# An attention-and-clustering kernel: the last MLP block of the third image computed in pieces during the fourth image's clustering

## The chip, the cores and the metric

The kernel runs on one core of a Trainium2 chip. The metric is the device time of one execution in microseconds (us). Before the change it is 3501.63 us, the median of three runs (3501.41 to 3505.16).

Engines are named as in the profile: PE multiplies matrices (PEld is its weight load), DVE is the vector engine, ACT the scalar engine, POOL the general-purpose engine, SP the engine whose queue issues most transfers. Each works through its own queue in order. Matmul results go to PSUM, everything else lives in SBUF.

## The reference

The input `x` is four images (B = 4) of 256 channels and 64 x 64 pixels, all float32. Two layers follow each other:

```python
# layer 0: attention over N = 4096 pixels
q = wq x + bq ; k = wk x + bk ; v = wv x + bv        # q, k: 32 channels; v: 256
attn = softmax(q k)
x = gamma * (v attn) + x

# layer 1
feat, val = conv1x1(group_norm(x), f_w), conv1x1(group_norm(x), v_w)     # 96 channels each
sim = sigmoid(beta + alpha * cosine(centres(feat), feat))                # per head and quarter image
sim = sim * one_hot(argmax(sim))
agg = (sim val + centres(val)) / (sum(one_hot) + 1)
y = x + ls1 * conv1x1(sim agg, proj_w)
y = y + ls2 * conv1x1(gelu(conv1x1(group_norm(y), mlp_w1)), mlp_w2)      # 256 -> 1024 -> 256
z = relu(batch_norm(y * dw_w))
z = relu(batch_norm(conv1x1(z, pw_w)))                                   # the output
```

Gelu is the tanh approximation, and each group norm runs over a whole image.

## The kernel before

The images go through three stages, one image after another. The order of every engine's instructions is the order of the program text (`manual_schedule`).

**Weighting** (`attention(b).weighting`) is the softmax and its product with `v`: 8 blocks of 512 output pixels by 8 groups of 512 input pixels, 64 units in all. A unit's scores (`score`) are computed 9 units ahead into a buffer of the ring `spool`, tag "s"; `exps` takes the row maximum off, exponentiates, and adds up the denominator on POOL; `weigh` is the product, line 406. Row maxima come from DVE maxima on the scores, `fold`, and `across`, which turns them on PE (`tt`) and builds a diagonal tile `dg` in the pool `work`; `spread` sends it to all partitions (`mb`). In its last units (`ahead`) it loads the next image into four tiles of the ring.

**Clustering** (`cluster`) has many short steps that follow each other: group norm statistics, centres, the products `fv` with the features, similarity (`similar`: a square root on ACT, a Tanh, and then the square root's table again through `table`), the choice of the best centre (`largest`, `weights`), counts (`cnt`), sums (`agg`), transposes (`tp`), projection (`gp`, `op`), and statistics (`seen`, `bn_stats`) for the second group norm. In between, `fill(n)` issues the next `n` pieces of the next image's projections: 32 pieces `v_half` (`vp`), two `k_half` (`kp`), one `q_four` (`qp`). There are 35 pieces; `weighting` takes 8 of them after its last unit, `group_norm` some, `cluster` the rest, and the start of `mlp` (`fill(N)`) whatever remains. The last image has no next one, so its list is empty.

**MLP** (`mlp`) takes the image in 8 blocks of 512 pixels. In a block, `first(nb, j)` computes the hidden groups j and j + 4 (128 channels each) with seven products of 128x256 in place of eight (`hp`, `hu`, `hq`, weights combined beforehand: `w1_s` holds C + D and −D in place of C and D, and `w_abcd`, `w_bac`, `w_bcd` are built on POOL). `second` adds their part of the second layer (`mo`), one group behind. `finish` adds the residue and makes the Relu, `last` does the output layer (`pw`), both one block behind. Evictions of ACT are put off through the list `hooks`, which the next `first` empties. `norm(nb + 1)` prepares the next block at the end of step (nb, 1), with two DVE instructions (line 971) and four subtracts on POOL, into a pair of rows in a ring buffer (`pairs`), which is also the staging buffer of the output transfer.

At the end of step (nb, 2) each block also computes one unit of the next image's scores (`nxt.score(nb, hooks, maxima)`), so that the next weighting finds its first eight units ready. A unit's four DVE maxima are put into `maxima`, and `rest(n)` issues them, two in each call of `first`. After the last block come `fold`, `maximum` (which calls `across`), and the first `exps`.

The ring `spool` has `N // XT + SLOTS` = 14 buffers of 8 KB a partition. It holds the x tiles (two blocks each, 4 an image; an image's tile becomes free when its second block is through `finish` and the Relu), scores, pairs, and the clustering's `vf` and `sim`. The pool `work` has a tag "w" of three rotating buffers (`dg`, `sg`, `cl`, the three combined weights). PSUM is in pools `ps_m` (two buffers), `ps_s` (two buffers of two banks: scores, `hq`, `pw`), and `ps_a` (accumulators).

Of the kernel before, what the change touches and what calls it, by code (L numbers as in the profile page):

```python
# [13 lines left out]
P = 128  # L14
# [3 lines left out]
NB = 512  # L18
# [27 lines left out]
def attention_then_cluster_block(  # L46
# [123 lines left out]
    def derived():  # L170
# [27 lines left out]
        nc.vector.tensor_copy(wf_t, tps[:ED, :C])  # L198
        nc.vector.tensor_copy(fvb[:, :ED], tps[:, C : C + ED])

    probe = const.tile([P, 1], F32, name="probe")
    nc.gpsimd.memset(probe, 1.0)

# [40 lines left out]
    def attention(b, xs):  # L244
# [115 lines left out]
            top = tops[nb]  # L360
            nc.vector.tensor_tensor(top[:, 0], top[:, 0], top[:, 1], ALU.max)

        def across(nb, tag="w", bufs=3):
            top = tops.pop(nb)
            tp = ps_m.tile([P, 4, P], F32, tag="m", name=f"tt_{b}_{nb}")
            for j in range(4):
                nc.tensor.transpose(tp[:, j, :], top[:, 0, j * P : (j + 1) * P], ident)  # L367
            mx = small.tile([P, 4], F32, tag="mx", name=f"mx_{b}_{nb}")
            nc.vector.tensor_reduce(mx, tp, AX.X, ALU.max)
            dg = work.tile([P, 4, P], F32, tag=tag, bufs=bufs, name=f"dg_{b}_{nb}")  # L370
            nc.vector.tensor_tensor(
                dg,
                ident.unsqueeze(1).to_broadcast([P, 4, P]),
                mx.unsqueeze(2).to_broadcast([P, 4, P]),
                ALU.mult,
            )
            return dg
# [108 lines left out]
            score(GRP)  # L486

        def maximum():
            half["dg"] = across(0, "rden", 1)

        def first():
            spread(0, half["dg"])
# [124 lines left out]

    h64_q = h64[:ED].rearrange("p (q h m) -> p q h m", q=4, h=HEADS)

    def cluster(b, ys, stats, cells, rest, fill):  # L620

        pool = small.tile([P, KC, 4, 4], F32, tag="pool", bufs=1, name=f"pool_{b}")

# [90 lines left out]
        ]  # L714
        prns = [small.tile([P, 64], F32, tag="prn", name=f"prn_{b}_{f}") for f in range(2)]

        sgs = [work.tile([P, NB // 2], F32, tag="w", bufs=3, name=f"sg_{b}_{f}") for f in range(2)]
# [14 lines left out]
        def similar(f, meanwhile=lambda: None):  # L732

            sg = sgs[f]
            rsqrt(prns[f], prns[f], L2_EPS, meanwhile)
            nc.vector.tensor_tensor(quad(sg), quad(sg), over_m(prns[f]), ALU.mult)
            nc.scalar.activation(sg, sg, AF.Tanh, scale=ab[:, 0:1], bias=ab[:, 1:2])
            if f == 0:
                table(AF.Sqrt)

        def largest(f):
# [81 lines left out]
        summed(lambda j, q: pool_w[:, j], True)  # L823
        heads(NBLK - 1)
        similar(1, lambda: fill(2))
        fill(3)
        table(AF.Sqrt)
        largest(1)
# [61 lines left out]
        def products(hb, c, qs):  # L890
            if c == 0:
                two = [
                    ps_s.tile([P, 2, NB], F32, tag="s", name=f"op_{b}_{hb}_{c}_{f}")
                    for f in range(2)
                ]
                ops = {q: two[q // 2][:, q % 2, :] for q in qs}
            else:
                ops = {
                    q: ps_a.tile([P, NB], F32, tag=f"a{q % 2}", name=f"op_{b}_{hb}_{c}_{q}")
                    for q in qs  # L900
                }
            for q in qs:
                rows = slice(q * 32, (q + 1) * 32)
                nc.tensor.matmul(  # L904
                    ops[q],
                    g_s[rows, c * P : (c + 1) * P],
                    sim_t[rows, hb, :],
                    start=True,
                    stop=True,
                )  # L910
            for q in qs:
                y = pieces[hb, c, q] = ys[2 * (q // 2) + hb][:, c, :].rearrange(
                    "p (h f w) -> p f h w", h=16, f=2
                )[:, q % 2]
                if c == 0:
                    nc.vector.scalar_tensor_tensor(
                        y,
                        ops[q].rearrange("p (h w) -> p h w", h=16),
                        par("ls1", c),
                        y,  # L920
                        ALU.mult,
                        ALU.add,
                    )
                else:
                    add = work.tile([P, NB], F32, tag="w", bufs=3, name=f"cl_{b}_{hb}_{q}")
# [19 lines left out]
        return stats2  # L945


    def mlp(b, ys, stats2, fill, nxt):


        w_bcd, w_bac, w_abcd = (
            work.tile([P, HID // 2], F32, tag="w", bufs=3, name=f"{n}_{b}")
            for n in ("w_bcd", "w_bac", "w_abcd")
        )
        nc.gpsimd.tensor_tensor(w_abcd, W_CD, W_A, ALU.subtract)
        nc.gpsimd.tensor_tensor(w_bac, w_abcd, W_D, ALU.add)
# [80 lines left out]
        def first(nb, j, todo):  # L1037


            e, f, g, h = quarters(pairs[nb][:, 0])  # L1040
            t2, t4, t3, _ = quarters(pairs[nb][:, 1])
            hs = work.tile([P, 2, NB], F32, tag=("t", "acc")[j % 2], bufs=1, name=f"hs_{b}_{nb}_{j}")
            h1, h2, h3, h4 = quarters(hs)
            u = ps_m.tile([P, NB], F32, tag="m", name=f"hu_{b}_{nb}_{j}")[:, :HB]
            p = ps_m.tile([P, NB], F32, tag="m", name=f"hp_{b}_{nb}_{j}")[:, :HB]
            q = ps_s.tile([P, 2, NB], F32, tag="s", name=f"hq_{b}_{nb}_{j}")[:, 0, :HB]
            act = AF.Gelu_apprx_tanh
            lo, hi = pvc("b1", P, j), pvc("b1", P, j + 4)

            def gelu(dst, src, bias):  # L1050
                nc.scalar.activation(dst, src, act, bias=bias)  # L1051

            def mo(n):
                for _ in range(n):
                    next(todo, None)

            def plus(dst, ps, term):
                nc.vector.tensor_tensor(dst, ps, term, ALU.add)  # L1058

            product(p, W_A, j, e)  # L1060
            nc.scalar.copy(h1, p)  # L1061
            product(u, w_abcd, j, t2)
            plus(h2, u, h1)
            hook()
            rest(2 if nb == NBLK - 1 and j == 3 else 1)
# [12 lines left out]
            plus(h3, u, h3)  # L1078
            gelu(h3, h3, hi)
            if nb == NBLK - 1 and j == 3:  # L1080
# [35 lines left out]
                maxima.pop(0)()  # L1116

        acc, todo = None, iter(())
        for nb in range(NBLK):
            for j in range(4):  # L1120
                hs = first(nb, j, todo)
                if j == 0:
                    if nb:
                        finish(nb - 1, acc)
                    acc = [
                        ps_a.tile([P, NB], F32, tag=f"a{c}", name=f"mo{c}_{b}_{nb}")
                        for c in range(KC)
                    ]
                if j == 1:
                    if nb:  # L1130
                        last(nb - 1)
                    if nb + 1 < NBLK:
                        norm(nb + 1, nc.gpsimd)
                if j == 2 and nxt:
                    nxt.score(nb, hooks, maxima)
                todo = second(nb, acc, hs, j)
        for _ in range(2):
            next(todo)
        if nxt:
            nxt.fold(0)  # L1140
            nxt.maximum()
        table(AF.Exp)
# [1 line left out]
            pass  # L1144
        if nxt:
            nxt.first()
        finish(NBLK - 1, acc)
        hook()
        if nxt:
            nxt.exps(0)  # L1150
        last(NBLK - 1)
        hook()

    def filler(todo):
        def fill(n):
# [5 lines left out]
    with tc.manual_schedule():  # L1161
        here = attention(0, xs0)
        here.alone()
        for b in range(B):
            xs1 = []
# [6 lines left out]
            fill = filler(list(nxt.projections) if nxt else [])  # L1172
            stats, cells, rest = here.weighting(ahead, fill, (lambda: None) if b else derived)
            stats2 = cluster(b, here.xs, stats, cells, rest, fill)
            mlp(b, here.xs, stats2, fill, nxt)
            here = nxt


# [74 lines left out]
```

## Time and profile before

| what | us |
|---|---|
| median of three runs | 3501.63 |
| profiled execution | 3501.59 |
| its span | 3499.7 |
| PE busy | 3427.0 (98%) |
| DVE busy | 2056.8 (59%) |
| ACT busy | 1681.1 (48%) |
| POOL busy | 1486.0 (42%) |

A profile is one execution, traced instruction by instruction. Times in it count from the span's start. A row of a timeline has the start, the duration, the engine, the line, the operation, the tile written and the tiles read, the shape, and the number of instructions merged into it; behind it, in brackets, how long the engine had been idle and what released it. Matmuls are pipelined, so the distance of two starts says more than a duration. The stages of the four images are easily found by their matmuls: `den` of line 576 opens what follows a weighting, `fv` (line 784) is the clustering, `hp` of line 1022 opens an MLP. Images are numbered from 0, as in the code: image 2 is the third and image 3 the last.

### The profile page before, as it was taken

The numbers are of one execution on the slowest core, as the hardware profiler recorded it, in microseconds if no ns is written. First come the engines' busy times: TensorE is split into PE (matmuls) and PEld (weight loads), VectorE is DVE, ScalarE is ACT, GpSimd is POOL, SyncE is SP. The second block draws the span as 40 slices with busy tenths as digits, with TensorE's granted clock in tenths as the row PEclk, the third lists the DMA queues.
The fourth block names the chain that finished last, engine by engine and source line by source line (L and its number), as shares of the span: only waits on it lengthen the run. The fifth ranks groups of instructions, "written<-read, shape, count | busy, mean of one in ns | idle before, by whom it ended". The sixth has DMA issues, their size and how long they took to land.

```text
span 3499.7 us, 31843 instructions
## 1 busy us (share of the span) xinstructions
PE 3427.0 (98%) x11784; PEld 1708.1 (49%) x11784; DVE 2056.8 (59%) x2944; ACT 1681.1 (48%) x2149; POOL 1486.0 (42%) x794
## 2 busy tenths in 40 slices
PE   8999999999999999999999999999999999997899
PEld 4444445656444444665544444465554444445565
DVE  4666664645566666465556666745546666664543
ACT  5545553444555554344455554534446455542344
POOL 2656664211265665420135665632104666572210
PEclk9999999999999999999999999999999999998999
DMA  2000001000000000000000000100000000000000
GB/s 91 6 4 3 7 0 48 7 19 19 16 3 4 3 7 18 31 7 19 19 16 4 3 7 3 40 9 13 19 12 15 4 7 3 4 0 1 6 19 24
DMA packets 25260, 47.16 MB, mean 13 GB/s; under 512 B 6704, under 2 KB 8592, under 8 KB 25104
## 3 DMA queue, kind: packets, MB, share of 16 engines
q1 hardware_dynamic: 20240, 38.29, 3.2%
q10 hardware_dynamic: 4608, 6.30, 0.8%
q8 instruction: 93, 1.52, 0.2%
q0 software_dynamic: 256, 0.52, 0.1%
q14 instruction: 63, 0.52, 0.0%
HBM read 19.93 MB, written 16.78 MB: 10 GB/s over the span
## 4 chain that ended last, share of the span: by engine, by line
PE 95%; DVE 3%; ACT 1%; issue 0%; DMA 0%; SPq 0%; ACTq 0%; DVEq 0%
PE av L406 51%; PE mo L1029 12%; PE sc L331 8%; PE hu L1022 4%; PE pw L998 3%; PE hq L1022 3%; PE hp L1022 3%; PE vp L283 2%; PE fv L784 2%; PE mb L381 1%; PE den L427 1%; PE op L904 1%; PE qp L302 0%; PE kp L260 0%; PE tt L367 0%
## 5 line engine op out<-in xcount | busy, mean ns | idle before, releaser
L406 PE MATMUL av<-s,v 128*128 128x512 f32 x4096 | 1826.6, 597 | 0.6 <-ACT s L396 0.6
L406 PEld LDWEIGHTS av<-s,v 128*128 128x128 f32 x4096 | 758.9, 190 | 1024.6 <-issue 1015.1
L401 POOL TENSOR_TENSOR acc<-acc,s 128x1024 f32<-128x1024 f32 x448 | 1057.8, 2361 | 467.4 <-ACT s L396 447.9
L396 ACT ACTIVATE s<-s 128x1024 f32<-128x1024 f32 x512 | 539.0, 1057 | 461.6 <-DVE s L393 428.1
L393 DVE TENSOR_TENSOR s<-s,mb 128x1024 f32<-128x1024 f32 x512 | 595.1, 1206 | 6.5 <-PE mb L381 6.5
L1029 PE MATMUL mo<-hs,w_s 128*128 128x512 f32 x1024 | 523.6, 594 | 4.3 <-ACT hs L1051 1.6
L353 DVE TENSOR_TENSOR top<-sc,top 128x1024 f32<-128x1024 f32 x196 | 239.9, 1224 | 388.0 <-PE sc L331 388.0
L1051 ACT ACTIVATE hs<-hs,pv_s 128x256 f32<-128x256 f32 x512 | 259.5, 508 | 367.6 <-DVE hs L1058 356.4
L349 ACT COPY s<-sc 128x1024 f32<-128x1024 f32 x224 | 226.1, 1009 | 350.8 <-PE sc L331 350.8
L1058 DVE TENSOR_TENSOR hs<-hu,hs 128x256 f32<-128x256 f32 x384 | 162.8, 424 | 368.1 <-ACT hs L1061 223.4
L984 POOL TENSOR_TENSOR xn<-xn 128x256 f32<-128x256 f32 x28 | 24.8, 884 | 703.7 <-DVE xn L971 453.6
L331 PE MATMUL sc<-q,k 32*128 32x512 f32 x2048 | 294.6, 640 | 0.0
L398 POOL TENSOR_TENSOR acc<-s 128x1024 f32<-128x1024 f32 x32 | 75.1, 2346 | 476.5 <-ACT s L396 476.5
L356 DVE TENSOR_TENSOR top<-sc,top 128x1024 f32<-128x1024 f32 x196 | 240.1, 1225 | 47.5 <-ACT s L349 30.9
L354 ACT COPY s<-sc 128x1024 f32<-128x1024 f32 x224 | 226.9, 1013 | 75.9 <-DVE top L353 39.8
L1058 DVE TENSOR_TENSOR hs<-hq,hs 128x256 f32<-128x256 f32 x384 | 151.1, 421 | 110.7 <-PE hq L1022 106.3
L1029 PEld LDWEIGHTS mo<-hs,w_s 128*128 128x128 f32 x1024 | 192.2, 190 | 44.7 <-ACT hs L1061 9.4
L331 PEld LDWEIGHTS sc<-q,k 32*128 32x128 f32 x2048 | 81.3, 182 | 191.4 <-issue 108.1
L1022 PE MATMUL hp<-xn,w_s 128*128 128x256 f32 x512 | 155.7, 386 | 4.5 <-DVE xn L971 4.5
L1022 PEld LDWEIGHTS hp<-xn,w_s 128*128 128x128 f32 x512 | 95.4, 191 | 76.8 <-issue 64.1
L283 PE MATMUL vp<-wv_s,x 128*128 128x256 f32 x512 | 123.3, 387 | 0.2 <-ACT v L291 0.2
L998 PE MATMUL pw<-xn,wpw_s 128*128 128x512 f32 x256 | 115.5, 594 | 2.2 <-ACT xn L1092 2.2
(198 smaller groups left out, 2799.0 us busy)
## 6 DMA issues: line engine op xcount, KB each, us to landing
x<-in_x SPq DMA_DIRECT2D x32, 512.0 KB, 4.6
out<-xn SPq DMA_DIRECT2D x64, 256.0 KB, 2.1
q<-q ACTq DMA_DIRECT2D x96, 64.0 KB, 2.0
w_s<-in_w SPq DMA_DIRECT2D x2, 1024.0 KB, 8.0
q<-q SPq DMA_DIRECT2D x24, 64.0 KB, 2.0
q<-q POOLq DMA_DIRECT2D x8, 64.0 KB, 6.2
wv_s<-in_wv SPq DMA_DIRECT2D x1, 256.0 KB, 7.3
wpw_s<-in_wpw SPq DMA_DIRECT2D x1, 256.0 KB, 10.4
```

The costliest lines, as they stand in the source:

```text
L331: nc.tensor.matmul(halves[r // 2][:, r % 2, :], k_s[rows, g, :], q_s[rows, :], start=True, stop=True)
L353: nc.vector.tensor_tensor(top, halves[1], top, ALU.max)
L354: nc.scalar.copy(s[:, 2:4, :], halves[1])
L356: nc.vector.tensor_tensor(top, halves[0], top, ALU.max)
L393: nc.vector.tensor_tensor(sh, sh, mxs[nb].unsqueeze(1).to_broadcast([P, 2, NB]), ALU.subtract)
L396: nc.scalar.activation(sh, sh, AF.Exp)
L401: nc.gpsimd.tensor_tensor(acc, acc, s[:, 2 * h : 2 * h + 2], ALU.add)
L406: nc.tensor.matmul(av[c], own["v"][:, RG * g + quarter, c * P : (c + 1) * P], slots[u][:, quarter, :], start=(g == 0 and quarter == 0), st ...
L1022: nc.tensor.matmul(out, w[:, j * P : (j + 1) * P], x, start=True, stop=True)
L1029: yield nc.tensor.matmul(acc[c], w2_s[:, jj, c * P : (c + 1) * P], hs[:, i], start=(j == 0 and i == 0), stop=(j == HID // P // 2 - 1 and i ...
L1051: nc.scalar.activation(dst, src, act, bias=bias)
L1058: nc.vector.tensor_tensor(dst, ps, term, ALU.add)
```

## The change

Image 2's MLP runs seven blocks in place of eight (`blocks`). Its last block's rows after clustering and the second group norm's factors are kept (`y` in `work` tags w0 and w1, `gab`), and `late_block` makes of that block a list of pieces that takes the place of the empty list in image 3's `fill`. `begin` prepares its input at the first call of `ahead` in image 3's weighting. The pieces are plain products of 512 columns: 16 for the hidden layer, 16 for the second layer, an empty one, and 4 for the output layer. Gelu is a separate step, four groups at a time, that `cluster` calls behind each of its two Tanh.

Besides, `similar` asks for Gelu's table ahead of Tanh, in every image; the rotating tag "w" becomes three tags w0 to w2 with one buffer each; and in image 2's MLP the eight units of scores are given to the seven blocks at other steps: (0, 2) to (4, 2) as before, then (5, 0), (6, 1) and (6, 2). Maxima that are left over are issued ahead of `fold`.

```diff
-        def across(nb, tag="w", bufs=3):
+        def across(nb, tag="w2"):
...
-            dg = work.tile([P, 4, P], F32, tag=tag, bufs=bufs, name=f"dg_{b}_{nb}")
+            dg = work.tile([P, 4, P], F32, tag=tag, bufs=1, name=f"dg_{b}_{nb}")
...
         def similar(f, meanwhile=lambda: None):
             sg = sgs[f]
             rsqrt(prns[f], prns[f], L2_EPS, meanwhile)
+            table(AF.Gelu_apprx_tanh)
             nc.vector.tensor_tensor(quad(sg), quad(sg), over_m(prns[f]), ALU.mult)
             nc.scalar.activation(sg, sg, AF.Tanh, scale=ab[:, 0:1], bias=ab[:, 1:2])
             if f == 0:
+                gelu(0)
                 table(AF.Sqrt)
...
         similar(1, lambda: fill(2))
+        gelu(1)
         fill(3)
         table(AF.Sqrt)
...
+    def late_block(b, y, gab):
...
+        def begin():
+            held["x"] = spool.tile([P, 2, KC, NB], F32, tag="s", name=f"xl_{b}")
+            held["y"] = spool.tile([P, 2, KC, NB], F32, tag="s", name=f"yl_{b}")
+            for k in range(KC):
+                nc.gpsimd.tensor_copy(held["y"][:, 0, k], y[k])
+                nc.scalar.activation(held["x"][:, 0, k], y[k], AF.Identity,
+                    scale=gab[:, k : k + 1], bias=gab[:, KC + k : KC + k + 1])
+            x = held["x"]
+            nc.gpsimd.tensor_tensor(x[:, 1, 0], x[:, 0, 0], x[:, 0, 1], ALU.subtract)
...
+        def first(j, k):
+            if k == 0:
+                if j % 4 == 0:
+                    held["h", j // 4] = spool.tile([P, 4, NB], F32, tag="s", name=f"hl_{b}_{j}")
+                held["p"] = ps_m.tile([P, NB], F32, tag="m", name=f"hlp_{b}_{j}")
+            x = held["x"]
+            nc.tensor.matmul(held["p"], w1_s[:, k, j * P : (j + 1) * P],
+                x[:, 1, 0] if k and j >= 4 else x[:, 0, k], start=(k == 0), stop=(k == KC - 1))
+            if k:
+                nc.scalar.activation(hidden(j), held["p"], AF.Identity, bias=pvc("b1", P, j))
+
+        def gelu(i):
+            for j in range(4 * i, 4 * i + 4):
+                nc.scalar.activation(hidden(j), hidden(j), AF.Gelu_apprx_tanh)
+
+        def second(j, c):
+            if j == 0:
+                held["a", c] = ps_m.tile([P, NB], F32, tag="m", name=f"mol_{b}_{c}")
+            nc.tensor.matmul(held["a", c], w2_s[:, j, c * P : (c + 1) * P], hidden(j),
+                start=(j == 0), stop=(j == HID // P - 1))
+            if j == HID // P - 1:
+                t = work.tile([P, NB], F32, tag=f"w{c}", bufs=1, name=f"tl_{b}_{c}")
+                nc.scalar.activation(t, held["a", c], AF.Identity, scale=par("ls2", c))
+                nc.gpsimd.tensor_tensor(held["y"][:, 0, c], held["y"][:, 0, c], t, ALU.add)
+                nc.scalar.activation(held["x"][:, 1, c], held["y"][:, 0, c], AF.Relu,
+                    scale=dw_d[:, c : c + 1], bias=dw_e[:, c : c + 1])
+
+        def last(c, k):
+            if k == 0:
+                held["p"] = ps_m.tile([P, NB], F32, tag="m", name=f"pwl_{b}_{c}")
+            x = held["x"]
+            nc.tensor.matmul(held["p"], wpw_s[:, k, c * P : (c + 1) * P], x[:, 1, k], ...)
+            if k:
+                nc.scalar.activation(x[:, 0, c], held["p"], AF.Relu, ...)
+                nc.sync.dma_start(out=ob[:, c, nb * NB : (nb + 1) * NB], in_=x[:, 0, c])
+
+        todo = [lambda j=j, k=k: first(j, k) for j in range(8) for k in range(KC)]
+        todo += [lambda j=j, c=c: second(j, c) for j in range(8) for c in range(KC)]
+        todo += [lambda: None]
+        todo += [lambda c=c, k=k: last(c, k) for c in range(KC) for k in range(KC)]
+        return begin, todo, gelu
+
-    def mlp(b, ys, stats2, fill, nxt):
+    def mlp(b, ys, stats2, fill, nxt, blocks):
...
-        for nb in range(NBLK):
+        if blocks == NBLK:
+            at = {(u, 2): u for u in range(GRP)}
+        else:
+            at = {(u, 2): u for u in range(5)} | {(5, 0): 5, (6, 1): 6, (6, 2): 7}
+        for nb in range(blocks):
             for j in range(4):
                 hs = first(nb, j, todo)
                 if j == 0:
...
+                if nxt and (nb, j) in at:
+                    nxt.score(at[nb, j], hooks, maxima)
                 if j == 1:
                     if nb:
                         last(nb - 1)
-                    if nb + 1 < NBLK:
+                    if nb + 1 < blocks:
                         norm(nb + 1, nc.gpsimd)
-                if j == 2 and nxt:
-                    nxt.score(nb, hooks, maxima)
                 todo = second(nb, acc, hs, j)
         for _ in range(2):
             next(todo)
         if nxt:
+            rest(len(maxima))
             nxt.fold(0)
             nxt.maximum()
...
+        if blocks < NBLK:
+            y = []
+            for k in range(KC):
+                y.append(work.tile([P, NB], F32, tag=f"w{k}", bufs=1, name=f"y_{b}_{k}"))
+                nc.gpsimd.tensor_copy(y[k], block(ys, k, NBLK - 1))
+            nc.gpsimd.tensor_copy(gab[:, :KC], ga)
+            nc.gpsimd.tensor_copy(gab[:, KC:], gb)
+            return late_block(b, y, gab)
...
             def ahead():
                 if nxt and len(xs1) < N // XT:
                     xs1.append(load_x(b + 1, len(xs1)))
+                elif late and not begun:
+                    begun.append(begin())
+
+            begin, todo, gelu = late or (None, list(nxt.projections) if nxt else [], lambda i: None)
+            fill = filler(todo)
...
+            late = mlp(b, here.xs, stats2, fill, nxt, NBLK - (b == B - 2))
```

More of the change, by code (lines that the diff above doesn't have):

```diff
@@ L199, in derived @@
         nc.vector.tensor_copy(fvb[:, :ED], tps[:, C : C + ED])
+    gab = const.tile([P, 2 * KC], F32, name="gab")
     probe = const.tile([P, 1], F32, name="probe")
@@ L488, in maximum @@
         def maximum():
-            half["dg"] = across(0, "rden", 1)
+            half["dg"] = across(0, "rden")
         def first():
@@ L618, in attention_then_cluster_block, with cluster @@
     h64_q = h64[:ED].rearrange("p (q h m) -> p q h m", q=4, h=HEADS)
-    def cluster(b, ys, stats, cells, rest, fill):
+    def cluster(b, ys, stats, cells, rest, fill, gelu):
         pool = small.tile([P, KC, 4, 4], F32, tag="pool", bufs=1, name=f"pool_{b}")
@@ L715, in cluster @@
         prns = [small.tile([P, 64], F32, tag="prn", name=f"prn_{b}_{f}") for f in range(2)]
-        sgs = [work.tile([P, NB // 2], F32, tag="w", bufs=3, name=f"sg_{b}_{f}") for f in range(2)]
+        sgs = [
+            work.tile([P, NB // 2], F32, tag=f"w{f}", bufs=1, name=f"sg_{b}_{f}") for f in range(2)
+        ]
         sim = spool.tile([P, 8, 4, 32], F32, tag="s", name=f"sim_{b}")
@@ L924, in products @@
                 else:
-                    add = work.tile([P, NB], F32, tag="w", bufs=3, name=f"cl_{b}_{hb}_{q}")
+                    add = work.tile(
+                        [P, NB], F32, tag=f"w{(4 * hb + q) % 3}", bufs=1, name=f"cl_{b}_{hb}_{q}"
+                    )
                     nc.scalar.activation(add, ops[q], AF.Identity, scale=par("ls1", c))
@@ L945, in cluster, with hidden @@
         return stats2
-    def mlp(b, ys, stats2, fill, nxt):
+    def late_block(b, y, gab):
+        nb = NBLK - 1
+        ob = out[b].rearrange("(k p) h w -> p k (h w)", p=P)
+        held = {}
+        def begin():
[3 more added lines that the diff above has]
+                nc.gpsimd.tensor_copy(held["y"][:, 0, k], y[k])
+                nc.scalar.activation(
+                    held["x"][:, 0, k],
+                    y[k],
+                    AF.Identity,
+                    scale=gab[:, k : k + 1],
+                    bias=gab[:, KC + k : KC + k + 1],
+                )
+            x = held["x"]
+            nc.gpsimd.tensor_tensor(x[:, 1, 0], x[:, 0, 0], x[:, 0, 1], ALU.subtract)
+        def hidden(j):
+            return held["h", j // 4][:, j % 4]
+        def first(j, k):
[4 more added lines that the diff above has]
+            x = held["x"]
+            nc.tensor.matmul(
+                held["p"],
+                w1_s[:, k, j * P : (j + 1) * P],
+                x[:, 1, 0] if k and j >= 4 else x[:, 0, k],
+                start=(k == 0),
+                stop=(k == KC - 1),
+            )
+            if k:
[6 more added lines that the diff above has]
+                held["a", c] = ps_m.tile([P, NB], F32, tag="m", name=f"mol_{b}_{c}")
+            nc.tensor.matmul(
+                held["a", c],
+                w2_s[:, j, c * P : (c + 1) * P],
+                hidden(j),
+                start=(j == 0),
+                stop=(j == HID // P - 1),
+            )
+            if j == HID // P - 1:
+                t = work.tile([P, NB], F32, tag=f"w{c}", bufs=1, name=f"tl_{b}_{c}")
+                nc.scalar.activation(t, held["a", c], AF.Identity, scale=par("ls2", c))
+                nc.gpsimd.tensor_tensor(held["y"][:, 0, c], held["y"][:, 0, c], t, ALU.add)
+                nc.scalar.activation(
+                    held["x"][:, 1, c],
+                    held["y"][:, 0, c],
+                    AF.Relu,
+                    scale=dw_d[:, c : c + 1],
+                    bias=dw_e[:, c : c + 1],
+                )
+        def last(c, k):
+            if k == 0:
+                held["p"] = ps_m.tile([P, NB], F32, tag="m", name=f"pwl_{b}_{c}")
+            x = held["x"]
+            nc.tensor.matmul(
+                held["p"],
+                wpw_s[:, k, c * P : (c + 1) * P],
+                x[:, 1, k],
+                start=(k == 0),
+                stop=(k == KC - 1),
+            )
+            if k:
+                nc.scalar.activation(
+                    x[:, 0, c],
+                    held["p"],
+                    AF.Relu,
+                    scale=pw_s[:, c : c + 1],
+                    bias=pw_e[:, c : c + 1],
+                )
+                nc.sync.dma_start(out=ob[:, c, nb * NB : (nb + 1) * NB], in_=x[:, 0, c])
[4 more added lines that the diff above has]
+        return begin, todo, gelu
@@ L951, in mlp @@
+    def mlp(b, ys, stats2, fill, nxt, blocks):
         w_bcd, w_bac, w_abcd = (
-            work.tile([P, HID // 2], F32, tag="w", bufs=3, name=f"{n}_{b}")
-            for n in ("w_bcd", "w_bac", "w_abcd")
+            work.tile([P, HID // 2], F32, tag=f"w{i}", bufs=1, name=f"{n}_{b}")
+            for i, n in enumerate(("w_bcd", "w_bac", "w_abcd"))
         )
@@ L1064, in first @@
             hook()
-            rest(2 if nb == NBLK - 1 and j == 3 else 1)
+            rest(2 if nb == blocks - 1 and j == 3 else 1)
             mo(1)
@@ L1079, in first @@
             gelu(h3, h3, hi)
-            if nb == NBLK - 1 and j == 3:
+            if nb == blocks - 1 and j == 3:
                 rest(1)
@@ L1146, in mlp @@
             nxt.first()
-        finish(NBLK - 1, acc)
+        finish(blocks - 1, acc)
         hook()
@@ L1150, in mlp @@
             nxt.exps(0)
-        last(NBLK - 1)
+        last(blocks - 1)
         hook()
+        if blocks < NBLK:
[6 more added lines that the diff above has]
+            return late_block(b, y, gab)
     def filler(todo):
@@ L1163, in attention_then_cluster_block @@
         here.alone()
+        late = None
         for b in range(B):
-            xs1 = []
+            xs1, begun = [], []
             nxt = attention(b + 1, xs1) if b + 1 < B else None
@@ L1170, in ahead @@
                     xs1.append(load_x(b + 1, len(xs1)))
-            fill = filler(list(nxt.projections) if nxt else [])
+                elif late and not begun:
+                    begun.append(begin())
+            begin, todo, gelu = late or (None, list(nxt.projections) if nxt else [], lambda i: None)
+            fill = filler(todo)
             stats, cells, rest = here.weighting(ahead, fill, (lambda: None) if b else derived)
-            stats2 = cluster(b, here.xs, stats, cells, rest, fill)
-            mlp(b, here.xs, stats2, fill, nxt)
+            stats2 = cluster(b, here.xs, stats, cells, rest, fill, gelu)
+            late = mlp(b, here.xs, stats2, fill, nxt, NBLK - (b == B - 2))
             here = nxt
```

## The prediction

> **What bounds the kernel now.** I read the page first, then the chain that ended last, then busy time and granted clock by stage, then PE's timeline in the stages that the change touches, and last the other engines there.
>
> ```profile
> span 3499.7 us, 31843 instructions
> PE 95%; DVE 3%; ACT 1%; issue 0%; DMA 0%; SPq 0%; ACTq 0%; DVEq 0%
> ...
> 1452.00:1534.00 82.00, 77.02 (x566) 61.09 (x565) 53.53 (x130) 37.40 (x60) 19.80 (x20) 0.98 0.03 7
> 2313.00:2395.00 82.00, 77.01 (x566) 61.32 (x565) 53.68 (x130) 37.56 (x60) 19.81 (x20) 0.98 0.03 7
> 3174.00:3256.00 82.00, 50.39 (x359) 41.98 (x357) 53.22 (x131) 27.69 (x42) 19.61 (x20) 0.75 0.00 1
> ```
>
> The last rows are the clustering of images 1, 2 and 3 (columns: stretch, length, busy time of PE, PEld, DVE, ACT, POOL, then granted clock). The chain is PE for 95%, so PE work that is moved into a PE hole is worth its full time. The one big hole is in the last row: 50 of 82 us busy, at clock 0.75, because image 3 has no successor whose projections could fill it. From `den` to the MLP's first `hp` image 2 takes 81.2 us (2313.62 to 2394.85) and image 3 takes 80.8 (3174.46 to 3255.25), so DVE's chain sets the length, filled or not.
>
> ```profile
> 2313.62 0.42 PE L576 MATMUL den<-rden,ones 128*32 128x128 f32 x8
> 2402.34 0.59 PE L1022 MATMUL hq<-xn,w_s 128*128 128x256 f32 x2
> ...
> 3174.46 0.43 PE L576 MATMUL den<-rden,ones 128*32 128x128 f32 x8
> 3263.87 0.59 PE L1022 MATMUL hq<-xn,w_s 128*128 128x256 f32 x2
> ...
> 2557.79 3.60 PE L998 MATMUL pw<-xn,wpw_s 128*128 128x512 f32 x8
> 2588.70 3.60 PE L998 MATMUL pw<-xn,wpw_s 128*128 128x512 f32 x8
> ...
> 3411.44 3.60 PE L998 MATMUL pw<-xn,wpw_s 128*128 128x512 f32 x8
> 3440.69 3.60 PE L998 MATMUL pw<-xn,wpw_s 128*128 128x512 f32 x8
> ```
>
> From `den` to the `hq` of the MLP's second hidden group, image 2 (filled) takes 2402.34 − 2313.62 = 88.72 us and image 3 (empty) 3263.87 − 3174.46 = 89.41. From one `pw` to the next, an MLP block takes 30.91 us in image 2, with its unit of scores, and 29.25 in image 3, without.
>
> **The change, part by part.** The sum starts at the profiled execution, 3501.59 us (span 3499.7 and 1.9 around it; the median of the three runs is 3501.63).
>
> *Block removed from image 2's MLP: −29.25.* The eight units of scores all stay, so the block goes at the price without scores. PE is busy 238.71 of 240 us there, so all of it is on the path.
>
> *The same block in the last clustering: −0.6.* It brings 36 matmuls of 512 columns, two passes of 0.43 us each: 36 × 0.86 = 31 us against a hole of 82 − 50 = 32. They go where images 0 to 2 issue 35 pieces: 32 of 0.86 and three of 1.8 (`kp`, `qp`). So image 2's stretch is the model: 88.72. The three long pieces stand beside DVE's 7.2 us of `bn_stats` there, so their lightness gives nothing. Two corrections. In image 2 the second Tanh starts 2.56 us after its Sqrt (2358.84 to 2361.40), since two `v` evictions stand between on ACT; in image 3 it is 1.57. The late pieces in that place evict nothing, so it becomes 1.57 and the added probe's 0.2: −0.8. At the MLP's start the late block's last eviction (as L1008, 0.78) comes behind the Gelu table on ACT, ahead of the first copy of `hp`, and it holds a `ps_m` buffer that `hu` or `hp` wants: +0.9. 88.72 − 0.8 + 0.9 = 88.8 against 89.41. Bounds: −1.5 (no eviction delay) to +2 (and PE starts as slowly as image 3 does now, 8.6 us from `hp` to that `hq` against 7.5).
>
> ACT's share of it, eight evictions, eight Gelu of 128x512 (bounds 0.69, L926, and 0.81, L644), two of each for the residue and Relu, is some 16 us in a stage where ACT is busy 28 of 82. Gelu's first four stand between Tanh (ends 3214.65) and the next Sqrt (3221.72): 4 × 0.8 + 1.5 for the table is 4.7 of 7.1 us. If that cover is gone, the Sqrt and all of DVE behind it is late by the excess. DVE gets nothing. POOL's two adds (L927, 1.28) come behind the clustering's own and ahead of `w_abcd`, which by image 2's rows then ends some 4 us ahead of its reader, `hu`; uncovered, up to 2.6. The two output DMAs (256 KB) go to SP's queue, which holds nothing else then.
>
> *Table: +0.6.* `table(Gelu)` ahead of each Tanh replaces Tanh's own load (1.28, L737) and adds a probe of 0.2 (L206). DVE waits for the second Tanh in each clustering: 3 × 0.2 for images 0 to 2. That Tanh runs under Gelu's table is not shown; if not, a second 1.28 comes in each: 4 × 1.28 = 5.1 is the upper bound, 0 the lower. I take the lower by the nearest row: the MLP's Copy (L1061) and Relu (L1092) run between Gelus with no load.
>
> A rule that speaks against it: the Trainium skill's "ScalarE: Activation LUTs", What ACT_TABLE_LOAD costs, has 1.28 us for the load and a drain of 1.38 behind it. Here Tanh starts 0.01 us after the load ends (3223.28, 3223.29), so I count 1.28; by the page four loads would cost 5.5 more.
>
> *`begin` and the kept rows: 0.* `begin` puts two copies and a subtract on POOL (128x512: 0.7 each by L117's width, 1.28 as L927, so up to 3.9) and two Identity on ACT, at unit 57. Behind them on POOL are the denominators' adds; the last gather ends at 3161.6 and `den` reads it at 3174.46, which covers them. The copies at image 2's end (up to 2.6) stand between the first two adds of image 3, where POOL idles 0.8 and then 1.9; they also free an x tile for unit 8's scores, copied at 2651.4. Uncovered, 0 to 1.3 each.
>
> *Scores packed tighter: +2.0.* Unit 6 now stands just ahead of `pw` of block 5. `pw` needs a `ps_s` buffer, and both hold scores. In unit 7 now, scores start at 2629.59, PE is done at 2630.66 and ACT's first copy (L339) runs from 2630.81 to 2631.82, so a buffer is free at some 2.3 us where PE wants `pw` at 1.1: +1.2. The second half leaves in the next hook, 0.4 too late for `hq`. At the end two maxima (0.68 each) are left over ahead of `fold`; the fold ends 1.4 later, and `tt` had 1.0 to spare: +0.4. Bounds 0 and 3.
>
> *The ring of large buffers: +4.0.* `spool` has 14. At the end of step (5, 1), `norm(6)` wants one while these live: 4 x tiles of image 3, 6 units of scores (unit 5 is now in at (5, 0), not (5, 2)), 2 x tiles of image 2 (blocks 4 to 7), and the pairs of blocks 4 and 5. That is 14 before the new one, where it was 13. The first to come free is block 4's pair, after its output DMA, which is issued in the next step:
>
> ```profile
> 2557.47 0.99 DVE L971 TENSOR_SCALAR xn<-x,ga_gn,gb_gn 128x512 f32<-128x512 f32 x2
> 2562.36 0.42 DVE L1058 TENSOR_TENSOR hs<-hu,hs 128x256 f32<-128x256 f32 x1 [3.89 <-ACT hs L1061]
> ...
> 2563.03 0.97 SPq L1011 DMA_DIRECT2D out<-xn  x2
> ...
> 2563.38 0.59 PE L1022 MATMUL hu<-xn,w_bac 128*128 128x256 f32 x2
> ```
>
> The first row is `norm(6)` now. The second DMA is issued at about 2563.5 and lands 2.1 us later (the page's DMA issues): 2565.7. `norm(6)` then takes 0.99, and the add queued behind it on DVE (with POOL's four subtracts, 12 us early) starts at 2566.7, not 2562.36: 4.3 late. PE's `hu` waits for that add and had 0.4 to spare: 3.9, some 4.0. PE has no slack to win it back. Lower bound 0 (a slot comes free earlier than I count); upper 5.6, if the idle PE also loses its clock: in image 3 `fv` takes 24.25 us against 22.61 after such holes.
>
> On the clock, "TensorE: Matmul & The Clock Gate", Part 1, says that an idle window of about 3.4 us halves the clock and as much work restores it. The trace agrees on the hole (0.75), and has no drop after a wait of 2.6 us in image 2. The page would add an estimated 1.7 us behind this stall; I add none.
>
> Sum: 3501.6 − 29.25 − 0.6 + 0.6 + 2.0 + 4.0 = 3478.4.
>
> **The rivals.**
> - *No ring wait.* For it: I count from the code, and the trace names no buffers. Against: the count before tops out at exactly 14. 3478.4 − 4.0 = 3474.4, or down to 3471.5 with the packed scores free. Chance 0.22.
> - *The pieces stretch the clustering.* ACT's order (evictions, Gelu, tables) makes DVE late. For it: DVE waits there for two Sqrt, two Tanh and the normalized blocks, all on ACT. Against: ACT idles 54 of 82 us. With the extra table, 3478.4 + 5.1 = 3483.5. Chance 0.13.
> - *Slower: the clock.* With no hole left, PE might be granted less over the whole span. Over 3427 busy us, 1% is 34 us; it decides from a mean clock of 0.985 in place of 0.992 (23 us lost), and at 0.98 gives 3478 + 41 = 3519. Against: PE is granted 1.00 through 240 us of full work in image 2. Chance 0.04.
> - *It does nothing.* The pieces wait for Gelu or buffers and come out at the end of the clustering instead of in it, 30 us late: about 3501. Against: every piece's inputs are ready before its place by the sums above. Chance 0.04.
>
> **How the numbers follow.** The forecast has 0.57. The time is its own, 3478.4. The range goes from the first rival's floor, 3471.5, to the second's 3483.5, rounded to 3484. A change within 0.2% (7 us) can't be told from none; faster has the first three cases, less what waits I have missed might eat: 0.92; same 0.04; slower 0.04.
>
> **What would show it.** Right: image 3's clustering at a clock near 0.97 and still about 82 us; seven `pw` groups in image 2's MLP; `norm(6)` on DVE (L971's successor) released by a DMA and `hu` waiting about 4 us once; `pw` of block 5 waiting for ACT about 1 us; as many table loads as before. Wrong: a Tanh behind two loads, `cnt` or `gnm` in image 3 waiting for ACT, or a wait in image 3's weighting for POOL.

## The result and the profile after

The changed kernel takes 3478.12 us (median of 4 runs, 3477.08 to 3479.77) where the kernel before took 3501.52 beside it (3500.15 to 3505.16): a ratio of 0.9932, 95% interval [0.9915, 0.9949]. The gain of 23.4 us is more than the 0.2% that can be told from nothing. The forecast was 3478.4 in a range of 3471.5 to 3484.0. The profiled execution took 3478.09. A second set of five runs, taken later beside the experiments, has its median at 3478.40.

The page first, its head and the shares of the chain that ended last:

```profile
span 3476.0 us, 31760 instructions
...
PE 94%; DVE 3%; ACT 1%; DMA 0%; issue 0%; SPq 0%; POOL 0%; ACTq 0%; DVEq 0%
```

PE sets the end as before. Next, windows of the changed kernel (columns: stretch, length, busy time of PE, PEld, DVE, ACT, POOL, then PE's granted clock, DMA share, GB/s): the last clustering, and a stretch in block 5 of image 2's MLP.

```profile
3151.00:3233.00 82.00, 75.31 (x430) 47.62 (x429) 56.51 (x134) 41.20 (x66) 22.28 (x22) 0.98 0.01 4
...
2566.70:2572.00 5.30, 5.22 (x9) 3.19 (x10) 2.76 (x7) 1.10 (x3) 2.73 (x4) 0.50 0.00 0
```

The last clustering is as long as it was, but PE is busy for 75 of 82 us in place of 50, at clock 0.98 in place of 0.75. In block 5 there is a stretch of 5.3 us at half clock, although PE is busy through all of it. Its cause is in the timelines, PE's first:

```profile
2557.25 3.60 PE L1102 MATMUL pw<-xn,wpw_s 128*128 128x512 f32 x8
...
2562.40 0.59 PE L1126 MATMUL hq<-xn,w_s 128*128 128x256 f32 x2
2566.78 1.22 PE L1126 MATMUL hu<-xn,w_bac 128*128 128x256 f32 x2 [3.78 <-DVE hs L1162]
...
2595.64 3.70 PE L1102 MATMUL pw<-xn,wpw_s 128*128 128x512 f32 x8 [1.15 <-ACT s L341]
...
3151.16 0.43 PE L578 MATMUL den<-rden,ones 128*32 128x128 f32 x8
...
3239.40 0.59 PE L1126 MATMUL hq<-xn,w_s 128*128 128x256 f32 x2
```

Then DVE, and SP's queue, in block 5:

```profile
2565.39 1.00 DVE L1075 TENSOR_SCALAR xn<-x,ga_gn,gb_gn 128x512 f32<-128x512 f32 x2 [7.78 <-DMA out<-xn]
2566.31 0.42 DVE L1162 TENSOR_TENSOR hs<-hu,hs 128x256 f32<-128x256 f32 x1
```

```profile
2562.48 0.97 SPq L1115 DMA_DIRECT2D out<-xn  x2
```

Read from the bottom: SP issues block 4's output transfer, `norm(6)` on DVE (line 1075) is released by that transfer, the add of line 1162 stands behind it in DVE's queue, and PE's `hu` waits 3.78 us for the add. A pair of `hu` that takes 0.59 at full clock then takes 1.22.

Stage by stage, from one image's `den` to the next, in the two profiled executions (the forecast's terms are put where they belong; the probes of images 0 and 1, the tiny activations that `table` issues behind a table load, make up the +0.4):

| stretch | before | after | difference | forecast |
|---|---|---|---|---|
| start to `den` of image 0 | 590.52 | 590.56 | +0.04 | 0 |
| `den` of image 0 to `den` of image 2 | 1723.10 | 1721.54 | −1.56 | +0.4 |
| `den` of image 2 to `den` of image 3 | 860.84 | 839.06 | −21.78 | −23.05 |
| `den` of image 3 to `hq` of the second hidden group | 89.41 | 88.24 | −1.17 | −0.6 |
| from there to the last `pw` | 227.38 | 227.38 | 0.00 | 0 |
| from there to the end | 8.45 | 9.22 | +0.77 | 0 |

The +0.77 at the end has no cause in the change that the trace shows; SP's issue of the last transfers takes 1.74 us there in place of 0.96. The forecast came within 0.3 us of the profiled execution, but that rests on errors of both signs, and the experiments were made to take them apart.

### The profile page after: what moved, and what is told of

Its sections match the earlier page's. It is cut to its first block, busy times and chain, and to the rows that moved or that the text cites. A ratio compares the mean times of both kernels' runs of the same rounds, so it can differ in the third digit from the quotient of the medians.

```text
span 3476.0 us, 31760 instructions
## 1 busy us (share of the span) xinstructions
PE 3421.1 (98%) x11760; PEld 1694.3 (49%) x11760; DVE 2046.2 (59%) x2912; ACT 1683.9 (48%) x2157; POOL 1489.2 (43%) x799
## 4 chain that ended last, share of the span: by engine, by line
PE 94%; DVE 3%; ACT 1%; DMA 0%; issue 0%; SPq 0%; POOL 0%; ACTq 0%; DVEq 0%
PE av L408 52%; PE mo L1133 12%; PE sc L333 8%; PE hu L1126 4%; PE pw L1102 3%; PE hp L1126 3%; PE hq L1126 3%; PE vp L285 2%; PE fv L790 2%; PE mb L383 1%; PE den L429 1%; PE op L911 1%; PE qp L304 0%; PE kp L262 0%; PE tt L369 0%
## 5 line engine op out<-in xcount | busy, mean ns | idle before, releaser
L1133 PE MATMUL mo<-hs,w_s 128*128 128x512 f32 x992 | 508.4, 596 | 3.8 <-ACT hs L1155 1.6
L1155 ACT ACTIVATE hs<-hs,pv_s 128x256 f32<-128x256 f32 x496 | 251.3, 508 | 360.9 <-DVE hs L1162 350.1
```

The costliest lines, as they stand in the source:

```text
L1133: yield nc.tensor.matmul(acc[c], w2_s[:, jj, c * P : (c + 1) * P], hs[:, i], start=(j == 0 and i == 0), stop=(j == HID // P // 2 - 1 and i ...
```

## The experiments

All edits are to the changed kernel unless something else is said. The kernel before takes 3501.76 us (median of 9 runs) beside the first four and 3500.56 (9 runs) beside the last three.

**Scores of unit 5 back in their old place.** With it, one buffer fewer is held when `norm(6)` wants one.

```diff
-            at = {(u, 2): u for u in range(5)} | {(5, 0): 5, (6, 1): 6, (6, 2): 7}
+            at = {(u, 2): u for u in range(6)} | {(6, 1): 6, (6, 2): 7}
```

> Only unit 5 of the scores goes back from step (5, 0) to (5, 2). Ring theory: at (5, 1) only 13 of the 14 large buffers live when norm(6) asks, so DVE's wait of 7.8 us for the output DMA goes, PE's 3.8 us before hu goes, and so does the half clock behind it (0.50 over the 5.3 us after the stall, worth 2.4): 3478.1 - 6.2 = 3471.9. Rival, the early scores only show a wait that is there anyway (DVE and ACT are too full in blocks 5 and 6 with eight units in seven blocks): the wait moves to block 6, 3476 to 3479.

Measured: 3476.34 us (3472.30 to 3479.79, 5 runs), ratio 0.9927 [0.9913, 0.9940]. By the median alone that is undecided, for it lies in the rival's range. The traced execution took 3472.30, near the 3471.9 of the ring theory. In its trace the transfer's wait at `norm(6)` and PE's wait of 3.78 are gone, and `den` of image 2 to `den` of image 3 takes 833.00 us, 6.06 less than in the changed kernel. The wait has not moved to block 6: from `pw` of block 5 to that of block 6 takes 24.13 us, against 24.14 in the changed kernel. The other four runs have no trace, so what makes them longer is not shown; their granted clock is lower (0.998 in the run of 3472.30, 0.996 in the next three, 0.995 in that of 3479.79).

**`norm(6)` later.** Everything stays where the change put it; `norm(6)` alone goes from the end of step (5, 1) to the end of (5, 2), when the transfer has landed.

```diff
-                    if nb + 1 < blocks:
+                    if nb + 1 < blocks and not (blocks < NBLK and nb == 5):
                         norm(nb + 1, nc.gpsimd)
+                if j == 2 and blocks < NBLK and nb == 5:
+                    norm(nb + 1, nc.gpsimd)
```

> Unit 5 stays at (5, 0); only norm(6) moves from the end of step (5, 1) to the end of (5, 2), behind the hook that issues block 4's output DMA. Ring theory: the buffer is asked for when it is about to be free, and the adds that PE waits for stand ahead of norm(6) on DVE, so PE's 3.8 us wait and the slow clock go: 3471.9, as with unit 5 put back. Rival, the packed scores themselves make DVE late: 3477 to 3479. If norm(6) then comes too late for block 6, hp of (6, 0) waits for DVE and the time lies between.

Measured: 3472.52 us (3469.94 to 3474.28, 4 runs), ratio 0.9914 [0.9900, 0.9928]. DVE in block 5, and the `pw` behind it on PE:

```profile
2565.57 0.42 DVE L1162 TENSOR_TENSOR hs<-hq,hs 128x256 f32<-128x256 f32 x1 [0.87 <-PE hq L1126]
...
2566.51 0.99 DVE L1075 TENSOR_SCALAR xn<-x,ga_gn,gb_gn 128x512 f32<-128x512 f32 x2
```

```profile
2585.69 1.14 PE L333 MATMUL sc<-q,k 32*128 32x512 f32 x8
2587.98 3.70 PE L1102 MATMUL pw<-xn,wpw_s 128*128 128x512 f32 x8 [1.15 <-ACT s L341]
```

Line 1075 has no bracket any more: it waits for nothing. `den` of image 2 to `den` of image 3 takes 832.29 (2311.21 to 3143.50), 6.77 less than in the changed kernel. So the ring's wait cost 6.8 us, not 3.8. The wait of `pw` is still 1.15, so it comes from the scores ahead of it and not from the ring. What is left over in this stretch is small: 860.84 before, less 29.25 for the block, is 831.59, and the kernel has 832.29, so the tighter scores and the Tanh's probe cost 0.7 together.

**PE kept busy through the wait.** Eight products that nothing reads go into the unused half of a PSUM buffer ahead of the `hu` that waits. They fill the wait without ending it, which separates the wait from what comes behind it.

```diff
             u = ps_m.tile([P, NB], F32, tag="m", name=f"hu_{b}_{nb}_{j}")[:, :HB]
-            p = ps_m.tile([P, NB], F32, tag="m", name=f"hp_{b}_{nb}_{j}")[:, :HB]
+            pt = ps_m.tile([P, NB], F32, tag="m", name=f"hp_{b}_{nb}_{j}")
+            p = pt[:, :HB]
...
             product(q, W_CD, j, f)
+            if blocks < NBLK and (nb, j) == (5, 2):
+                for _ in range(8):
+                    nc.tensor.matmul(pt[:, HB:], ones, e, start=True, stop=True)
             product(u, w_bac, j, t3)
```

> The changed kernel with 8 more products of 128x256 (3.4 us, into an unused half of hp's bank, read by nobody) on PE in step (5, 2), just ahead of the hu that waits 3.8 us. Clock theory: PE is busy through the stall, the clock stays at 1.00 behind it, and the kernel gains what the half clock cost, 2.4: 3475.7. Rival, what is slow behind the stall is the backlog of DVE and ACT and not the clock: 3478, or 3478.5 if the products run a little over the stall.

Measured: 3478.18 us (3477.62 to 3479.50, 5 runs); by the total, what the rival expected. PE's timeline and the window behind the wait:

```profile
2564.47 0.59 PE L1126 MATMUL hp<-xn,w_s 128*128 128x256 f32 x2
...
2566.62 3.62 PE L1175 MATMUL hp<-xn,ones 128*128 128x256 f32 x16
2570.57 0.70 PE L1126 MATMUL hu<-xn,w_bac 128*128 128x256 f32 x2 [0.33 <-DVE hs L1163]
```

```profile
2570.00:2576.00 6.00, 5.67 (x21) 3.68 (x20) 4.27 (x10) 2.37 (x5) 3.24 (x4) 1.00 0.00 0
```

From the step's `hp` to that `hu` is 6.10 us here and 6.10 in the changed kernel (2560.68 to 2566.78): the wait for the add is the same. Behind it the clock is 1.00 in place of 0.50, and from `hu` to the `pw` of block 5 takes 26.16 us in place of 28.86. So 2.70 us of the 6.8 are half clock, which PE gets because it stood idle. The theory holds for this stage, but its 3475.7 for the total was missed. In the traced execution (3478.82) other stages are longer than in the changed kernel's and outweigh the gain: 2.07 up to `den` of image 0, 1.53 in image 0 and 1.47 from `den` to `hp` in image 2, where `cnt` to the first `tp` takes 5.48 us in place of 4.54; image 1 is 1.27 shorter. The other four runs have no trace, so for their totals the cause stays open.

**All pieces at the end.** The late block's pieces are held back until the last MLP begins, where the fill of what remains takes them in one go. The work is the same; it no longer lies in the hole.

```diff
-    def filler(todo):
+    def filler(todo, held_back):
         def fill(n):
+            if held_back and n < N:
+                return
...
-            fill = filler(todo)
+            fill = filler(todo, late is not None)
```

(The two groups of Gelu go into the list behind the first 16 pieces, and the two `tl` tiles get other buffers.)

> The same late block, but all its pieces are held back and issued together at the start of the last image's MLP; the clustering stays empty. Hole theory: the change gains because PE has 31 us free in that clustering, so here the 31 us come on top, with some 4 to 7 us of waits for Gelu and the Relu between the pieces, and the clustering falls back to a clock of 0.75 (1.2 us): 3510 to 3518, slower than before the change. Rival, the gain is mainly the shorter MLP and its scores packed tighter, and the late block would be hidden wherever it stands: 3478 to 3490.

Measured: 3519.93 us (3518.96 and 3520.89), ratio 1.0050 [1.0032, 1.0068], a little over what the theory expected and far from the rival. `den` of image 3 to the `hq` takes 128.17 us, 39.9 more. Its PE timeline shows where:

```profile
3229.77 0.56 PE L216 MATMUL gnm_gn<-mv_gn,left 128*128 128x1 f32 x2 [8.33 <-DVE mv_gn L214]
...
3231.77 15.61 PE L988 MATMUL hlp<-xl,w_s 128*128 128x512 f32 x32
3248.67 14.00 PE L1005 MATMUL mol<-hl,w_s 128*128 128x512 f32 x32 [1.29 <-ACT hl L1000]
3264.78 1.12 PE L1028 MATMUL pwl<-xl,wpw_s 128*128 128x512 f32 x2 [2.10 <-ACT xl L1016]
3267.53 5.34 PE L1028 MATMUL pwl<-xl,wpw_s 128*128 128x512 f32 x6 [1.63 <-ACT xl L1016]
```

Laid end to end, the pieces take 36 us of PE, where 31 were counted, and 5 of waits for ACT, and DVE's chain ahead of them is as long as ever (`gnm` waits 8.33 for it). In the hole all of it is free (88.24 us, against 89.41 without the block). The change therefore lives from where the pieces stand.

**A wait in every clustering filled.** Image 2's `cnt` waits 2.7 us on DVE and comes out of it at a reduced clock. On top of "`norm(6)` later", three pieces move from among the last products into that wait:

```diff
         gelu(1)
-        fill(3)
+        fill(6)
...
-        fill(2)
+        fill(1)
         products(0, 1, (2, 3))
-        fill(2)
+        fill(0)
...
-        fill(2)
+        fill(1)
         products(1, 1, (2, 3))
```

> The changed kernel with norm(6) at the end of stage (5,2) as in the kernel e4_norm_later (3472.5 us), and besides, in every clustering, three of the next image's pieces (or of the late block's) moved from among the last products to the wait before cnt: fill(3) becomes fill(6), the three fill(2) become 1, 0 and 1. Theory (PE falls to half clock when it waits 2.7 us before cnt, and the products after it pay for it; how much depends on a phase): the wait before cnt falls from 2.70 to about 0.2 in images 0 to 2 (3 x 0.93) and from 1.74 to about 0.3 in the last; cnt to the first tp takes about 3.0 us in all four, where it took 4.53, 5.47, 4.54 and 2.96; the places that lose pieces are set by DVE, which the pieces only covered; so about 4 to 6 us less, 3467 to 3469. Rival 1 (the clock does not depend on that wait): cnt to tp stays between 2.9 and 5.5, and the time stays at 3472 to 3473. Rival 2 (the pieces taken away leave as long a wait at the products, which PE pays): each clustering loses 1.9 us there, and the time is 3472 or above although cnt to tp is short.

The same move in the kernel before, which has no pieces in its last clustering:

> The kernel before with the same move of three pieces into the wait before cnt, and nothing else; the last image has no pieces there, so only images 0 to 2 can gain. Theory (clock after a wait): cnt to tp 3.0 us in images 0 to 2, where it was 5.43, 4.30 and 4.55 in the profile of before: 3 to 5 us less, 3497 to 3499; the last image keeps its wait of 2.6 us and takes 2.9 to 5.5 us. Rival (the clock does not depend on the wait, or the moved pieces cost elsewhere what they bring): 3500 to 3503.

And the changed kernel beside them:

> The changed kernel itself, beside the two others on one chip. Both theories: 3477 to 3480; the distance to e6_fill_moved is then the stall in block 5 (about 6) and the half clock before cnt (4 to 6), so 10 to 12 us by the theory and about 6 by the rival.

Measured: 3458.18 us (3456.17 to 3458.76, 4 runs), ratio 0.9877 [0.9862, 0.9893]; in the kernel before 3488.56 (3486.51 to 3489.72, 5 runs), ratio 0.9965 [0.9953, 0.9978]; the changed kernel 3478.40 (3477.95 to 3483.98, 5 runs). Both moves bring more than any of the expectations. PE's timeline, image 2, with the wait (`norm(6)` later) and without (the filled kernel):

```profile
2362.34 2.04 PE L841 MATMUL cnt<-scr,ones 128*96 128x64 f32 x16 [2.70 <-DVE scr L760]
...
2366.88 0.66 PE L859 MATMUL tp<-ident,sim 128*128 128x128 f32 x4
```

```profile
2348.41 7.17 PE L285 MATMUL vp<-wv_s,x 128*128 128x256 f32 x32
2355.70 1.57 PE L841 MATMUL cnt<-scr,ones 128*96 128x64 f32 x16
...
2358.66 0.65 PE L859 MATMUL tp<-ident,sim 128*128 128x128 f32 x4
```

| image 2 (us) | `norm(6)` later | filled |
|---|---|---|
| `den` to `cnt` | 51.13 | 51.13 |
| `cnt` to the first `tp` | 4.54 | 2.96 |
| first `tp` to `gnm` | 21.50 | 19.40 |
| `gnm` to the MLP's first `hp` | 4.14 | 3.76 |

The clock part is as the theory had it: `cnt` to `tp` is 2.96 us in images 0 to 2 of both filled kernels, and 2.89 in the last image of the filled changed kernel, where it was 4.53, 5.47, 4.54 and 2.96. But the theory was wrong about the rest. The stretch behind `tp` isn't set by DVE in images 0 to 2: PE had no wait in it and was the bound itself, so three pieces fewer made it 2.1 us shorter, until `gnm` waits 0.84 for DVE. In the last image PE already waited 3.20 at `gnm`, so there the move gives only 0.3 from `den` to `hp` (81.07 to 80.77). The sum over the images, `den` to `den`, is 4.06, 5.47 and 4.07, and 0.3: 13.9; 5.7 of it is `cnt` to `tp`, that is, clock. The two traced executions differ by only 11.2 (3469.94 and 3458.76), since the one with `norm(6)` later reached `den` of image 0 2.9 earlier. Between the medians it is 14.3, but these come from two sets of runs in which the kernel before differs by 1.2.

In the kernel before, images 0 to 2 become 5.55, 4.07 and 4.10 shorter. The last image becomes 1.63 longer from `den` to `hp`, with nothing changed in it. The expectation had its wait wrong: ahead of `cnt` PE waits 6.13 us there before and 5.85 here, not 2.6, and `cnt` to `tp` takes 5.47 both times.

The filled changed kernel is the fastest version of all, 42.4 us below the kernel before it ran beside.

Not tried: a ring of 15 buffers; the tighter scores alone with all eight blocks; and another place for unit 6, so that `pw` doesn't wait its 1.15.

## Why the prediction was right, step by step

- **The block removed, −29.25: right.** With the ring's wait out of the way the stretch of image 2 falls by 28.55, which is 29.25 less the 0.7 of the scores and the probe.
- **The block in the hole, −0.6: right in that the pieces fit, and in part lucky in size.** `den` to `hq` is 88.24 against a forecast of 88.8, and the kernel with the pieces at the end shows what the hole hides. The parts are not those of the sum, though. Against image 2 of the same execution (88.81), the last image is 0.99 shorter up to `cnt` (forecast 0.8) and 0.30 shorter from `hp` to `hq`, where 0.9 more was forecast. Two differences that no term had nearly cancel. `cnt` to `tp` is 1.58 shorter, since the clock stays at 1.00 behind the wait of 1.74. `gnm` to `hp` is 2.53 longer (6.67 against 4.14): the last four pieces (`pwl`) stand there, and behind `gnm`'s wait of 3.20 the clock is 0.50 from 3227.62 to 3231.03. From `tp` to `gnm` it is 0.22 shorter.
- **"DVE's chain sets the length, filled or not": wrong for images 0 to 2.** With three pieces taken out from behind `tp`, the stretch from there to `gnm` fell from 21.50 to 19.40, so PE's own work set it. For the last image it holds up to `gnm`, where PE waits for DVE.
- **Eight Gelu on ACT: fewer us than counted.** ACT's eight Gelu were priced at 0.8 each and take 0.54 (four in 2.17):

```profile
3196.66 1.28 ACT L208 ACT_TABLE_LOAD   x1
3197.95 0.20 ACT L208 ACTIVATE probe<-probe 128x1 f32<-128x1 f32 x1
3198.06 0.58 ACT L742 ACTIVATE sg<-sg,ab 128x256 f32<-128x256 f32 x1
3198.55 2.17 ACT L1000 ACTIVATE hl<-hl 128x512 f32<-128x512 f32 x4
```

- **Table, +0.6: right, mis-sized.** These rows of the last clustering (ACT of the changed kernel) have one load and then Tanh and Gelu behind it with no other, so the lower bound was the one to take; there are 31 loads in both kernels. The probe delays Tanh by 0.1, not 0.2. The Trainium skill's "ScalarE: Activation LUTs", What ACT_TABLE_LOAD costs, counts a drain of 1.38 us on top of a load. It shows on neither side of this one: the load starts 0.02 us after ACT's instruction before it has ended (3196.64), and the probe 0.01 us after the load.
- **`begin`, the kept rows, POOL's adds: 0, right.** No wait for POOL stands ahead of PE; the last combined weight is done at 3230.2, before the MLP's first `hp` at 3232.22.
- **Scores packed tighter, +2.0: too much.** The wait of `pw` came as forecast (1.15 against 1.2, released by the copy that I named), but `hq` is only 0.25 late and `tt` 0.17, where 0.4 each was forecast, and a second unit in one stretch costs less than a block's own: from `pw` of block 3 to that of block 4 takes 31.79 us with two units, where 30.91 is the time with one and 29.25 without. The net is some 0.6.
- **The ring, +4.0: the step that failed, by its size.** Mechanism, place and wait were right (14 buffers, `norm(6)` released by block 4's transfer, 3.78 us against 4.0). It cost 6.8, since 2.7 us of half clock followed (the kernel with PE kept busy) and 0.3 are not accounted for. I had put the clock at nothing with the words "has no drop after a wait of 2.6 us in image 2". That was a misreading: the mean of the 82 us (0.98) hides the stretch behind the wait. The two kernels' windows there, before and after:

```profile
2364.60:2369.30 4.70, 4.63 (x81) 4.37 (x82) 1.42 (x5) 0.00 (x0) 0.00 (x0) 0.64 0.02 3
```

```profile
2364.60:2369.30 4.70, 4.68 (x79) 4.15 (x79) 1.21 (x4) 1.06 (x3) 0.00 (x0) 0.70 0.02 3
```

  A clock of 0.64 was in the trace of before. The rule that I set aside ("TensorE: Matmul & The Clock Gate", Part 1) would have added an estimated 1.7 and was right in direction; the upper bound of 5.6 was still below the 6.8.
- **Luck in the total.** Images 0 and 1 came out 1.56 shorter where +0.4 was due. Of that, 2.48 less and 1.17 more is `cnt` to `tp`, which goes by where the wait falls in the clock's periods and not by the change (last section). Ring and scores together were forecast at 6.0 and cost 7.4, and this hid the difference.
- **The rivals.** "No ring wait" is refuted by the trace, yet it is what the two kernels without the wait show (832.29 and 833.00 for the stretch). Its floor doesn't follow from the sum given: 3474.4 less the 2.0 of the scores is 3472.4, and 3471.5 is reached only with 0.9 more, the bound without the eviction delay. "The pieces stretch the clustering" and "it does nothing" are refuted by the 88.24, and "the clock over the whole span" by a granted clock of 0.997, against 0.992 before.

## What to carry to other kernels

A wait on PE costs its length and can cost half clock behind it: up to 3.1 us behind a wait of 2.7 here, and nothing behind 1.74. So read the granted clock of the few microseconds after each wait, not the mean of the stage. When a program is filled from a list of independent pieces, put them where PE waits for another engine and take them out of stretches in which PE itself is the bound, even if those are only a few products apart. And count ring buffers at each step that asks for one: a step moved up by half a block turned an output transfer into PE's releaser.

## What the hardware showed that was not expected

The same wait can halve the clock or leave it alone. In one execution of the changed kernel, `cnt` waits 2.71 us in image 0 and 2.70 in image 1. These are its windows from `cnt` to the first `tp` (image 0, image 1), and then windows of 3.41 us and 6.83 us around the two waits:

```profile
641.71:644.66 2.95, 2.95 (x80) 2.74 (x80) 1.39 (x4) 0.00 (x0) 0.00 (x0) 1.00 0.00 0
1501.04:1506.51 5.47, 5.47 (x80) 5.08 (x81) 1.39 (x4) 0.00 (x0) 0.00 (x0) 0.50 0.00 0
...
640.32:643.73 3.41, 2.02 (x41) 1.96 (x45) 2.07 (x6) 0.69 (x2) 0.00 (x0) 1.00 0.00 0
...
1497.06:1500.48 3.42, 1.27 (x6) 0.77 (x5) 1.94 (x5) 3.26 (x6) 0.00 (x0) 1.00 0.00 0
1500.48:1507.31 6.83, 6.27 (x84) 5.88 (x85) 1.88 (x6) 0.24 (x1) 0.00 (x0) 0.50 0.00 0
1507.31:1510.72 3.41, 3.39 (x23) 2.28 (x23) 0.22 (x1) 2.09 (x4) 0.00 (x0) 1.00 0.02 5
```

The same products take 2.95 us at clock 1.00 and 5.47 at 0.50. What differs is where the wait falls. Within each trace the clock changes only at moments that lie multiples of 3.413 us apart: in the changed kernel's MLPs and clusterings at 1500.48, 1507.31, 2364.05, 2367.46, 2565.44, 2572.27, 3227.62 and 3231.03 (from 1500.48 to 2364.05 it is 253 times 3.413). So time is cut into periods of 3.413 us, and each is at full or at half clock as a whole. The boundary at 640.32 splits image 0's wait into 1.32 and 1.39 us. Of image 1's wait 2.14 us lie in the period that ends at 1500.48, and the two periods behind it are at half clock. Every wait of over 1 us ahead of `cnt` in the nine profiles goes by its largest part in one period:

| wait (us) | largest part in one period | cases | clock behind it | `cnt` to `tp` |
|---|---|---|---|---|
| 1.74 | 0.89 to 1.36 | 5 | 1.00 | 2.96 |
| 2.70 to 2.71 | 1.39 to 1.88 | 4 | 1.00 | 2.95 to 2.96 |
| 2.61 to 2.71 | 2.04 to 2.71 | 17 | 0.50 for one period (10) or two (7) | 4.29 to 5.48 |
| 5.85 to 6.13 | 3.15 to 3.41 | 3 | 0.50 before the wait ended | 5.47 |

With no wait, or one of 0.11 at most, it is 2.89 to 2.96 in seven cases. From `cnt` to `gnm`, half clock for one period costs 1.5 to 1.6 us behind a wait of 2.7, and for two periods 2.9 to 3.1. Elsewhere the limit is less sharp: in the second profile of the changed kernel a period in the last clustering with PE busy for 0.42 of it left the clock alone, and the next one, with 0.47, halved it. What else counts is not shown.

The periods don't keep step with the program: in the two profiles of the changed kernel the boundary stands 1.39 and 1.21 us ahead of image 0's `cnt`. Whether this is also most of what makes runs of one kernel differ by some 3 us is not shown; the filled changed kernel, which has no wait over 0.11 ahead of `cnt`, still spreads by 2.59. A change of 5 us is in any case better read from stages of the trace than from the total.

The Trainium skill's "TensorE: Matmul & The Clock Gate", Part 1, describes a free-running window of about 3.4 us, which would make the outcome depend on where a wait falls. The traces agree, with periods of 3.413 us. The page's section Why this matters for your kernels asks for no idle gaps over about 3 us, and here gaps of 2.7 already cost up to 3.1 us.
